# PSUM laid out by hand in the attention of a transformer block: three score tiles late, one bank for side work, chains two pairs ahead

## The chip, the core and the metric

The kernel runs on one core of one Trainium2 chip. A core has five engines that run side by side, each through its own instructions in order: TensorE (PE in the profile, its weight loads PEld), VectorE (DVE), ScalarE (ACT), GpSimd (POOL) and SyncE (SP, which here only issues DMAs). Work passes between them through SBUF (the large on-chip memory) and PSUM (where matmuls write). The metric is the device time of the whole kernel in microseconds; smaller is better.

## What is computed

A block of four layers over x of 4 sequences x 1024 tokens x 256 features, fp32, each with a layer norm ahead and a residual around it: attention, a mixture of experts, a causal convolution over the batch axis, and the same mixture again.

```python
x = x + _L0_attn_a_ref(_layernorm(x, axis=-1), L0_attn_a_w_qkv, L0_attn_a_w_out, L0_attn_a_ln_scale, L0_attn_a_ln_bias)
x = x + _L0_ffn_ref(_layernorm(x, axis=-1), L0_ffn_gate_w, L0_ffn_w1, L0_ffn_w2, L0_ffn_shared_w1, L0_ffn_shared_w2)
x = x + _L0_attn_b_ref(_layernorm(x, axis=-1), L0_attn_b_delta, L0_attn_b_alpha, L0_attn_b_beta, L0_attn_b_gamma)
x = x + _L0_ffn_ref(_layernorm(x, axis=-1), L0_ffn_gate_w, L0_ffn_w1, L0_ffn_w2, L0_ffn_shared_w1, L0_ffn_shared_w2)
```

The change is in the attention: 16 heads of 16 features, q and k rotated and normalised per head, and then weights that are the fourth power of the score instead of an exponential.

```python
def polynomial_attention(q, k, v, degree, is_causal):
    a = jnp.einsum('bhnd,bhmd->bhnm', q, k) ** degree
    if is_causal:
        a = jnp.tril(a)
    denom = jnp.sum(a, axis=-1, keepdims=True)
    return jnp.einsum('bhnm,bhmd->bhnd', a / denom, v)
```

The experts' part (16 experts, 6 per token, and a shared one) needs the tokens sorted by expert: the kernel scatters normalised rows into a queue in DRAM.

## The kernel before

**Passes and steps.** A sequence and a half of the heads (8 of 16) make a pair; there are 8 pairs. Queries come in two halves of 512 tokens (`hf`): first all 8 pairs with the early half, which sees keys of 4 blocks of 128, then all with the late half, which sees 8. One pair with one half is a pass (16 of them). A pass treats its 8 heads as two head-halves `a` of 4 heads, and for each walks over the key blocks `j`. So an early pass has 2 x 4 = 8 steps and a late one 2 x 8 = 16: 64 early steps and 128 late ones. Key blocks on the diagonal (the last four) are narrower and need a causal mask.

**One step.** `scores` (L686) lets PE multiply one key block with the queries of 4 heads into two PSUM tiles of 128 x 2 x 512 (L694); ACT squares both into SBUF (L705). On the diagonal DVE masks the first by a product (L712) and POOL the second (L714). Then the squares are squared again, to the fourth power: the first tile's on DVE (L725), the second's on ACT a step later (L863), some early ones on POOL (L727). `weigh` (L734) lets PE multiply these with v, with a column of ones for the sum, into an accumulator (L742). After the last block ACT copies that to SBUF (L751). Scores run `LOOK` = 2 steps ahead of weighing, in the main loop (L856).

**Side work in bites.** Everything else of the attention stage is cut into generators that run a piece at a time between the steps, in five lanes: `qkv_bites` of the pairs of either head group (L552; a chain of four projections, rotation, centring, square root, scaling, two times four transposes with an affine), `norm_bites` (the norm of x and its transposes), `gather_bites` with `project_bites` (division, output projection and residual), and a lane for routing (`prepare`, `plan`, `scatter`: norm, gate logits, top-k, slots and the 96 scatters of the first group). A generator yields `"pe"` ahead of a piece with matmuls, `"el"` ahead of one without, and `"gap"` where it wants to wait for the next step. `Bites.step(pe, counts)` runs at most so many pieces in each lane, and at most `pe` with matmuls in all. The loop calls it twice in a step, once after the scores and once after the weighing, both with `pe` = 1. `begin_chain(n)` starts the chain of pass n, `need` finishes it by force.

**What sets the order.** PE, DVE, ACT and SP keep the order in which the code is written; POOL's order comes from the scheduler of the framework. An engine waits for another through a semaphore, and everything behind a waiting instruction waits as well.

**PSUM.** Eight banks of 128 x 512 fp32: pool `ps_s` with two score tiles of two banks, `ps_a` with one accumulator, `ps_m` with three banks for bites, in both halves.

**Chains.** In the early half the chain of pass n + 2 begins at the middle of pass n, in the late half that of pass n + 1 at j = 3 of the first head-half of pass n. There is one v buffer for each pair of the early half, and two, used in turn, in the late one.

**After the attention.** The pools are given back and the experts' stage takes their memory: on SP loads of the shared experts' weights (L903, L906) and the gate and up weights (L911), on ACT loads of `w2a` and `w2b` (L918, L922), on DVE two memsets in `w2b` (L920, L921). Then the shared experts of the first group run (`shared`, L930), whose first matmuls (L955) need `hxT`, a transposed copy (L946), and only then the stream of routed tiles.

Of the kernel before, what the change touches and what calls it, by code (L numbers as in the profile page):

```python
# [8 lines left out]
FP = mybir.dt.float32  # L9
# [88 lines left out]
def chain(*parts):  # L98
    for part in parts:
        yield from part  # L100
# [3 lines left out]
def block_kernel(  # L104
# [342 lines left out]
    with ExitStack() as actx:  # L447
# [48 lines left out]
        def v_buffer(name):  # L496
            va = ap1.tile([P, 4, 8 * VW + 16], FP, name=name)
            nc.gpsimd.memset(va, 1.0)
            return va

        vA = [v_buffer(f"vA{i}") for i in range(len(pairs))]
        vB = [v_buffer(f"vB{i}") for i in range(2)]
        kA = [ap1.tile([P, 512], FP, name=f"kA{i}") for i in range(len(pairs))]


# [11 lines left out]
                    )  # L517

        qT, kT, vs_of, at_of, xnT_of = {}, {}, {}, {}, {}
        PS = {}  # L520

        def ps_m():
            return PS["m"]
# [1 line left out]
        def norm_bites(l, hf):  # L525

            xs = X[:, 4 * hf : 4 * hf + 4, l, :]
            yield "el"
            mv = small.tile([P, 4, 2], FP, tag="a_mv", name="a_mv")
            rstd = small.tile([P, 4], FP, tag="a_rstd", name="a_rstd")  # L530
            ln_stats(xs, mv, "a")
            yield "gap"
            yield "el"
            ln_root(mv, rstd)
            yield "gap"
            yield "el"
            nc.vector.reciprocal(rstd, rstd)
            xn = ap1.tile([P, 4, E], FP, name="xn")
            ln_apply(xs, xn, mv, rstd)
            xnT = ap2.tile([P, 2, 512], FP, name="xnT")  # L540
            xnT_of[l, hf] = xnT
            yield "gap"
            yield "gap"
            for k in range(2):
                yield "pe"
                pt = ps_m().tile([P, 512], FP, tag="m", name="pt")
                transpose4(pt, xn, slice(k * P, (k + 1) * P))
                nc.scalar.copy(xnT[:, k, :], pt)
# [3 lines left out]
        def qkv_bites(u, hf):  # L552
# [1 line left out]
            n = hf * len(pairs) + u  # L554
            l, gp = pairs[u]
            xnT = xnT_of[l, hf]
            va = vA[u] if hf == 0 else vB[u % 2]
            hd = D // 2
            full = [P, 2, 16, D]
            half = [P, 2, 16, hd]  # L560
# [125 lines left out]
        def scores(u, hf, a, j, last):  # L686

            n0 = max(0, (j - 4 * hf) * P)
            nq = 512 - n0
            kt = kT[u, j // 4]  # L690
            tiles = [PS["s"].tile([P, 2, 512], FP, tag="s", name="ps") for _ in range(2)]

            for h in (2, 0, 1, 3):
                nc.tensor.matmul(  # L694
                    tiles[h // 2][:, h % 2, 0:nq],
                    lhsT=kt[32 * h : 32 * h + 32, (j % 4) * P : (j % 4 + 1) * P],
                    rhs=qT[u, hf][a][32 * h : 32 * h + 32, n0:512],
                    start=True,
                    stop=True,
                )  # L700
            s2s, later = [], []
            masked = j >= 4 * hf
            for pr in range(2):
                s2 = sqp.tile([P, 2, 512], FP, name="s2")
                nc.scalar.activation(s2[:, :, 0:nq], tiles[pr][:, :, 0:nq], AF.Square)  # L705
                s2s.append(s2)
            for pr in range(2):
                s2 = s2s[pr]
                if masked:

                    if pr == 0:
                        nc.vector.tensor_mul(s2[:, :, 0:P], s2[:, :, 0:P], seen)  # L712
                    else:
                        nc.gpsimd.affine_select(  # L714
                            out=s2[:, :, 0:P],
                            in_=s2[:, :, 0:P],
                            compare_op=ALU.is_ge,
                            fill=0.0,
                            base=0,
                            pattern=[[0, 2], [1, P]],  # L720
                            channel_multiplier=-1,
                        )
                part = s2[:, :, 0:nq]
                if pr == 0 and (hf == 1 or j % 2 == 0):
                    nc.vector.tensor_mul(part, part, part)  # L725
                elif pr == 1 and hf == 0 and j % 2 == 1:
                    nc.gpsimd.tensor_mul(part, part, part)  # L727
                else:
                    later.append(part)
            return s2s, later  # L730

        accs = {}

        def weigh(u, hf, a, j, last, s2s):  # L734
            n0 = max(0, (j - 4 * hf) * P)
            if j == 0:
                accs[0] = PS["a"].tile([P, 512], FP, tag="acc", name="acc")
            acc = accs[0]
            va = vs_of[u, j // 4]
            for r in (2, 0, 1, 3):  # L740
                h = 2 * r + a
                nc.tensor.matmul(  # L742
                    acc[32 * r : 32 * r + 32, n0:512],
                    lhsT=va[:, j % 4, h * VW : h * VW + 32],
                    rhs=s2s[r // 2][:, r % 2, 0 : 512 - n0],
                    start=(j == 0),
                    stop=(j == last),
                )
# [82 lines left out]
        def forward(i):  # L831

            n, a, j, last = steps[i]
            hf, u = passes[n]
            if a == 0 and j == 0:
                bites.need(pairs[u][1], n)
            if hf == 0 and a == 1 and j == 0:
                begin_chain(n + 2)
            if hf == 1 and u > 0 and a == 0 and j == 3 and n + 1 < len(passes):

                begin_chain(n + 1)
            return scores(u, hf, a, j, last)

        with tc.manual_schedule(engines=ORDERED):
            with tc.tile_pool(name="ps_s", bufs=2, space=PSUM) as s, tc.tile_pool(
                name="ps_a", bufs=1, space=PSUM
            ) as a, tc.tile_pool(name="ps_m", bufs=3, space=PSUM) as m:
                PS.update(s=s, a=a, m=m)
                bites.add(NORM, norm_bites(0, 0), (0, 0))
                begin_chain(0)  # L850
                bites.need(QKV0, 0)
                begin_chain(1)
                bites.add(ROUTE, taps(ap1, ps_m))
                bites.add(ROUTE, zero_fill())
                routed = False
                for s in range(-LOOK, len(steps)):  # L856
                    bites.begin()
                    new = []
                    if s + LOOK < len(steps):
                        powers[s + LOOK], new = forward(s + LOOK)  # L860
                    bites.step(1, (1, 1, 1, 1, 1))
                    for part in later:
                        nc.scalar.activation(part, part, AF.Square)  # L863
                    later[:] = new
                    if s < 0:
                        bites.step(1, (2, 2, 1, 2, 1))
                        continue
                    n, a, j, last = steps[s]
                    hf, u = passes[n]
                    o_sb = weigh(u, hf, a, j, last, powers.pop(s))  # L870
                    bites.step(1, (2, 2, 1, 2, 1 if 0 not in plans or s % 2 else 0))
                    if o_sb is not None:
                        l, gp = pairs[u]
                        done = gather_bites(u, hf, a, o_sb)
                        if gp == 1 and a == 1:
                            done = chain(done, project_bites(l, hf))
                        bites.add(OUT, done)
                    if hf == 1 and not routed and not bites.lanes[OUT]:

                        routed = True  # L880
                        for i in range(TG):
                            bites.add(ROUTE, prepare(0, i, ap1, ps_m))
                        bites.add(ROUTE, chain(plan(0, ps_m), scatter(0, ap2, 1)))
                bites.drain(OUT)
                bites.drain(ROUTE)


    with ExitStack() as fctx:
# [432 lines left out]
```

## Time and profile before

| | us |
|---|---|
| median of 3 runs | 2390.59 (2389.18 to 2391.22) |
| the profiled execution, its run | 2393.24 |
| the profiled execution, its span | 2391.5 |
| attention, early half | 35 to 275 |
| attention, late half | 275 to 761 |
| shared experts of the first group | 761 to 855 |
| the rest (routed experts, convolution, experts again) | 855 to 2391.5 |

Busy in the whole span: PE 2114.5 us (88%), DVE 1118.5 (47%), ACT 1240.2 (52%), POOL 901.4 (38%). Mean granted clock of TensorE: 0.925.

How to read the lines of the profile that follow below: a group names line, engine, operation and output<-input, how often, and then busy time and mean duration in ns; after the bar stands the idle time of the engine ahead of it and what ended it. A line of the timeline begins with its start and length in us, and ends in brackets with the idle time and the releaser. A line of the waits names who waited for whom, us in total, times, and the longest.

### The profile page before, as it was taken

The page shows a single profiled execution, that of the slowest core. Times are in us where ns is not written, and L with a number is a line of the kernel's source. Part 1 is how long each engine was busy: PE and PEld are TensorE (multiplying, and loading weights), DVE is VectorE, ACT ScalarE, POOL GpSimd, SP SyncE. Part 2 cuts the span into 40 slices and gives each one's busy share as a digit, 9 for nine tenths or more (in the row PEclk, how much of TensorE's full clock was granted, in tenths as well). Part 3 has the DMA queues.
Part 4 walks back from the last instruction along what each step waited for, and adds up shares of the span by engine and source line. Part 5 has one row for each costly group of instructions (what it writes and reads, how often), then busy time and mean ns, then how long its engine had stood idle before and what let it go on. Part 6 is the DMA issues. An engine that isn't in the chain of part 4 may idle for free.

```text
span 2391.5 us, 33033 instructions
## 1 busy us (share of the span) xinstructions
PE 2114.5 (88%) x10480; PEld 1308.4 (55%) x10480; DVE 1118.5 (47%) x2532; ACT 1240.2 (52%) x2754; POOL 901.4 (38%) x990
## 2 busy tenths in 40 slices
PE   5899999778898998999899999789999959999974
PEld 2344443222233466777666667567676747777632
DVE  5888867656555225111166652126754212441154
ACT  3677878566676145555455544335553424555410
POOL 3333211344431000444355226645513654540176
PEclk8888988889888999999999999989999979999987
DMA  7900000111101412555455335344423535663243
GB/s 232 342 7 1 1 1 1 38 51 45 53 27 62 114 48 79 165 166 166 137 151 154 102 104 176 132 139 142 145 92 121 176 124 154 202 186 115 91 123 112
DMA packets 212231, 267.73 MB, mean 112 GB/s; under 512 B 25280, under 2 KB 187232, under 8 KB 212064
## 3 DMA queue, kind: packets, MB, share of 16 engines
q1 hardware_dynamic: 166944, 161.04, 21.6%
q0 software_dynamic: 36992, 100.78, 13.4%
q10 hardware_dynamic: 8128, 3.80, 0.7%
q8 instruction: 91, 1.49, 0.3%
q14 instruction: 76, 0.62, 0.1%
HBM read 123.72 MB, written 141.82 MB: 111 GB/s over the span
## 4 chain that ended last, share of the span: by engine, by line
PE 67%; DVE 12%; issue 7%; ACT 7%; POOL 5%; DMA 2%; ACTq 0%; POOLq 0%; DVEq 0%; SPq 0%
PE pgu L1030 20%; PE py L1053 14%; PE ps L694 6%; PE acc L742 4%; PE pxt L1014 4%; PE pht L1044 4%; POOL xq L421 3%; PE pg L955 3%; ACT s L705 3%; PE pj L571 3%; PE pu L955 3%; PE po L972 3%; POOL yg L1147 2%; ACT s L863 1%; DVE X L1131 1%
## 5 line engine op out<-in xcount | busy, mean ns | idle before, releaser
L421 POOL DMA_INDIRECT xq<-sxn,sloti x384 | 379.2, 987 | 644.7 <-ACT xgT L1016 306.2
L1030 PE MATMUL pgu<-wgu,xgT 128*128 x1776 | 609.7, 466 | 4.4 <-DVE hbuf L1039 2.2
L1147 POOL DMA_INDIRECT yg<-yq,sloti x384 | 375.8, 979 | 421.8 <-issue 201.4
L1039 DVE TENSOR_TENSOR hbuf<-hbuf,pgu 128x176 f32<-128x176 f32 x444 | 149.4, 337 | 721.7 <-ACT hbuf L1038 721.2
L1030 PEld LDWEIGHTS pgu<-wgu,xgT 128*128 128x128 f32 x1776 | 338.7, 193 | 136.5 <-issue 20.3
L1038 ACT ACTIVATE hbuf<-pgu 128x176 f32<-128x176 f32 x444 | 141.4, 318 | 411.7 <-PE pgu L1030 411.6
L705 ACT ACTIVATE s<-ps 128x1024 f32<-128x1024 f32 (+3 forms) x384 | 291.4, 815 | 114.6 <-PE ps L694 113.5
L1053 PE MATMUL py<-w2a,hT 128*128 x888 | 268.7, 385 | 0.9 <-ACT yo L1062 0.9
L1053 PE MATMUL py<-w2b,hT 128*128 x888 | 266.4, 382 | 0.0
L1062 ACT COPY yo<-py 128x256 f32<-128x256 f32 x444 | 166.1, 374 | 167.0 <-PE py L1053 166.7
L1131 DVE SCALAR_TENSOR_TENSOR X<-yg,top,X 128x256 f32<-128x256 f32 x384 | 186.0, 484 | 87.8 <-DMA yg<-yq,sloti 81.8
L1014 PE MATMUL pxt<-ident,xg 128*128 128x128 f32 x888 | 171.8, 276 | 60.6 <-DMA xg<-xq 60.6
L714 POOL TENSOR_SCALAR_AFFINE_SELECT s<-s 128x256 f32<-128x256 f32 x128 | 84.2, 659 | 349.7 <-ACT s L705 349.5
L725 DVE TENSOR_TENSOR s<-s 128x1024 f32<-128x1024 f32 (+3 forms) x160 | 168.2, 1051 | 86.8 <-ACT s L705 83.5
L1016 ACT COPY xgT<-pxt 128x256 f32<-128x256 f32 x444 | 167.9, 378 | 68.7 <-PE pxt L1014 68.3
L694 PE MATMUL ps<-q,kA 32*128 32x512 f32 (+3 forms) x1024 | 182.0, 647 | 20.0 <-ACT s L705 18.0
L1044 PEld LDWEIGHTS pht<-ident,hbuf 128*128 128x128 f32 x888 | 125.9, 142 | 124.4 <-issue 71.1
L1053 PEld LDWEIGHTS py<-w2b,hT 128*128 128x128 f32 x888 | 170.2, 192 | 23.5
L863 ACT ACTIVATE s<-s 128x1024 f32<-128x1024 f32 x192 | 164.4, 856 | 27.5 <-POOL s L714 27.2
L1044 PE MATMUL pht<-ident,hbuf 128*128 128x128 f32 x888 | 171.6, 275 | 4.9 <-ACT hT L1046 4.9
L1046 ACT COPY hT<-pht 128x256 f32<-128x256 f32 x444 | 165.4, 372 | 1.7 <-PE pxt L1014 0.7
L742 PE MATMUL acc<-s,vA 128*32 128x512 f32 (+3 forms) x1024 | 140.1, 603 | 13.2 <-ACT s L863 10.8
(158 smaller groups left out, 2421.9 us busy)
## 6 DMA issues: line engine op xcount, KB each, us to landing
xg<-xq SPq DMA_DIRECT2D x148, 384.0 KB, 3.7
yq<-yo SPq DMA_DIRECT2D x148, 384.0 KB, 2.8
xq<-zero SPq DMA_DIRECT2D x74, 384.0 KB, 4.6
xq<-sxn,sloti POOLq DMA_INDIRECT x384, 2.4
yg<-yq,sloti POOLq DMA_INDIRECT x384, 2.9
wgu<-in_w SPq DMA_DIRECT2D x4, 1408.0 KB, 17.8
X<-in_x SPq DMA_DIRECT2D x8, 512.0 KB, 5.5
out<-X SPq DMA_DIRECT2D x8, 512.0 KB, 3.5
```

The source lines that it names most:

```text
L421: d = nc.gpsimd.indirect_dma_start(out=xq[g][:, :], out_offset=bass.IndirectOffsetOnAxis(ap=sloti[:, c + i, k : k + 1], axis=0), in_=xs[:, ...
L694: nc.tensor.matmul(tiles[h // 2][:, h % 2, 0:nq], lhsT=kt[32 * h : 32 * h + 32, (j % 4) * P : (j % 4 + 1) * P], rhs=qT[u, hf][a][32 * h : ...
L705: nc.scalar.activation(s2[:, :, 0:nq], tiles[pr][:, :, 0:nq], AF.Square)
L725: nc.vector.tensor_mul(part, part, part)
L742: nc.tensor.matmul(acc[32 * r : 32 * r + 32, n0:512], lhsT=va[:, j % 4, h * VW : h * VW + 32], rhs=s2s[r // 2][:, r % 2, 0 : 512 - n0], st ...
L863: nc.scalar.activation(part, part, AF.Square)
L1014: nc.tensor.transpose(pt[:, k, :], xg[c][:, k * P : (k + 1) * P], ident)
L1030: nc.tensor.matmul(pg, lhsT=xT[c][:, k, :], rhs=wgu_f[k][:, bass.ds(vals[0] * (2 * FI), 2 * FI)], start=(k == 0), stop=(k == 1),)
L1044: nc.tensor.transpose(pt[:, k, :], hbuf[c % 4][:, k * P : (k + 1) * P], ident)
L1053: nc.tensor.matmul(py, lhsT=hT[c][:, k, :], rhs=w2_f[k][:, bass.ds(off[c] * E, E)], start=(k == 0), stop=(k == 1),)
L1131: nc.vector.scalar_tensor_tensor(X[:, t, l, :], yg[:, k, :], top[:, i, k0 + k : k0 + k + 1], X[:, t, l, :], op0=ALU.mult, op1=ALU.add,)
L1147: nc.gpsimd.indirect_dma_start(out=yg[:, k, :], out_offset=None, in_=yq[g][:, :], in_offset=bass.IndirectOffsetOnAxis(ap=sloti[:, i, k0 + ...
```

## The change

Three parts. PSUM is laid out by hand: three score tiles, one bank `sums` and one bank `spare`. In the early half two score tiles are used, and bites rotate over `spare` and the two banks of the third tile; in the late half the three score tiles are used in turn (`turn`), and bites have `spare` alone. In the late half the first call of `step` gets `pe` = 0, so that a step runs at most one bite with matmuls, after the weighing. The fourth power of the second tile moves from ACT to DVE in the late half for j = 1 and 3. Late chains begin two passes ahead (at j = 6 of the second head-half of pass n for pass n + 2), with three v buffers in turn. The main loop keeps its content and loses a level of indentation.

```diff
-        vB = [v_buffer(f"vB{i}") for i in range(2)]
+        vB = [v_buffer(f"vB{i}") for i in range(3)]
...
+        pp = actx.enter_context(tc.tile_pool(name="psum", bufs=1, space=PSUM))
+        score_tiles = [pp.tile([P, 2, 512], FP, name=f"sc{i}") for i in range(3)]
+        sums = pp.tile([P, 512], FP, name="sums")
+        spare = pp.tile([P, 512], FP, name="spare")
+
+        class Banks:
+            def __init__(self, banks):
+                self.banks, self.n = banks, 0
+            def tile(self, shape, dtype, tag=None, name=None):
+                bank = self.banks[self.n % len(self.banks)]
+                self.n += 1
...
+                view = bank[:, 0:size]
...
+                return view
+
+        early = Banks([spare, score_tiles[2][:, 0, :], score_tiles[2][:, 1, :]])
+        late = Banks([spare])
+        PS = {"m": early}
+        turn = [0]
...
-            va = vA[u] if hf == 0 else vB[u % 2]
+            va = vA[u] if hf == 0 else vB[u % 3]
...
-            tiles = [PS["s"].tile([P, 2, 512], FP, tag="s", name="ps") for _ in range(2)]
+            tiles = []
+            for _ in range(2):
+                tiles.append(score_tiles[turn[0] % (2 if hf == 0 else 3)])
+                turn[0] += 1
...
-                if pr == 0 and (hf == 1 or j % 2 == 0):
+                if pr == 0 and (hf == 1 or j % 2 == 0) or hf == 1 and j in (1, 3):
                     nc.vector.tensor_mul(part, part, part)
...
-            if j == 0:
-                accs[0] = PS["a"].tile([P, 512], FP, tag="acc", name="acc")
-            acc = accs[0]
+            acc = sums
...
-            if hf == 1 and u > 0 and a == 0 and j == 3 and n + 1 < len(passes):
-
-                begin_chain(n + 1)
+            if hf == 1 and a == 1 and j == 6 and n + 2 < len(passes):
+
+                begin_chain(n + 2)
+            if hf == 1:
+                PS["m"] = late
...
-                    bites.step(1, (1, 1, 1, 1, 1))
+                bites.step(0 if PS["m"] is late else 1, (1, 1, 1, 1, 1))
```

More of the change, by code (lines that the diff above doesn't have):

```diff
@@ L519, in block_kernel @@
         qT, kT, vs_of, at_of, xnT_of = {}, {}, {}, {}, {}
-        PS = {}
+        pp = actx.enter_context(tc.tile_pool(name="psum", bufs=1, space=PSUM))
[8 more added lines that the diff above has]
+                self.n += 1
+                size = 1
+                for d in shape[1:]:
+                    size *= d
+                view = bank[:, 0:size]
+                if len(shape) == 3:
+                    view = view.rearrange("p (a b) -> p a b", b=shape[2])
+                elif len(shape) == 4:
+                    view = view.rearrange("p (a b c) -> p a b c", b=shape[2], c=shape[3])
+                return view
[3 more added lines that the diff above has]
+        turn = [0]
         def ps_m():
@@ L730, in scores @@
             return s2s, later
-        accs = {}
         def weigh(u, hf, a, j, last, s2s):
             n0 = max(0, (j - 4 * hf) * P)
-            if j == 0:
-                accs[0] = PS["a"].tile([P, 512], FP, tag="acc", name="acc")
-            acc = accs[0]
+            acc = sums
             va = vs_of[u, j // 4]
@@ L838, in forward @@
                 begin_chain(n + 2)
-            if hf == 1 and u > 0 and a == 0 and j == 3 and n + 1 < len(passes):
-                begin_chain(n + 1)
+            if hf == 1 and a == 1 and j == 6 and n + 2 < len(passes):
+                begin_chain(n + 2)
+            if hf == 1:
+                PS["m"] = late
             return scores(u, hf, a, j, last)
         with tc.manual_schedule(engines=ORDERED):
[L845 to L860, printed above, removed]
-                    bites.step(1, (1, 1, 1, 1, 1))
[L862 to L885, printed above, removed]
@@ new lines, in block_kernel @@
+            bites.add(NORM, norm_bites(0, 0), (0, 0))
+            begin_chain(0)
+            bites.need(QKV0, 0)
+            begin_chain(1)
+            bites.add(ROUTE, taps(ap1, ps_m))
+            bites.add(ROUTE, zero_fill())
+            routed = False
+            for s in range(-LOOK, len(steps)):
+                bites.begin()
+                new = []
+                if s + LOOK < len(steps):
+                    powers[s + LOOK], new = forward(s + LOOK)
+                bites.step(0 if PS["m"] is late else 1, (1, 1, 1, 1, 1))
+                for part in later:
+                    nc.scalar.activation(part, part, AF.Square)
+                later[:] = new
+                if s < 0:
+                    bites.step(1, (2, 2, 1, 2, 1))
+                    continue
+                n, a, j, last = steps[s]
+                hf, u = passes[n]
+                o_sb = weigh(u, hf, a, j, last, powers.pop(s))
+                bites.step(1, (2, 2, 1, 2, 1 if 0 not in plans or s % 2 else 0))
+                if o_sb is not None:
+                    l, gp = pairs[u]
+                    done = gather_bites(u, hf, a, o_sb)
+                    if gp == 1 and a == 1:
+                        done = chain(done, project_bites(l, hf))
+                    bites.add(OUT, done)
+                if hf == 1 and not routed and not bites.lanes[OUT]:
+                    routed = True
+                    for i in range(TG):
+                        bites.add(ROUTE, prepare(0, i, ap1, ps_m))
+                    bites.add(ROUTE, chain(plan(0, ps_m), scatter(0, ap2, 1)))
@@ L888, in block_kernel @@
+            bites.drain(OUT)
+            bites.drain(ROUTE)
     with ExitStack() as fctx:
```

## The prediction

> **What bounds the kernel now.** I read the busy times of each engine in three stretches first, then the chain of waits, then the late half step by step.
>
> ```profile
> 35.00:275.00 240.00, 217.24 (x1400) 94.48 (x1396) 198.03 (x376) 171.97 (x297) 85.70 (x114) 0.89 0.38 125
> 275.00:761.00 486.00, 416.93 (x2496) 146.40 (x2492) 297.76 (x535) 354.43 (x485) 149.17 (x173) 0.87 0.08 27
> 761.00:855.00 94.00, 83.39 (x257) 46.19 (x258) 28.40 (x46) 14.68 (x26) 0.00 (x0) 0.91 0.42 112
> ...
> 400.00:447.00 47.00, 42.53 (x252) 16.07 (x248) 43.40 (x71) 36.80 (x50) 4.13 (x7) 0.97 0.00 1
> 447.00:475.00 28.00, 19.01 (x92) 5.01 (x84) 10.99 (x19) 11.59 (x16) 17.63 (x19) 0.63 0.19 69
> ```
>
> Columns: stretch, its length, then busy us of PE, weight loads, DVE, ACT and POOL, TensorE clock, DMA share, GB/s. Attention is 35 to 761 us: the early half to 275, the late half 486 us for 128 steps. The shared experts then run to 855 us. After 761 us the change touches nothing but when the stage may begin. In the chain of waits PE carries two thirds:
>
> ```profile
> PE 67%; DVE 12%; issue 7%; ACT 7%; POOL 5%; DMA 2%; ACTq 0%; POOLq 0%; DVEq 0%; SPq 0%
> ```
>
> In the late half that is PE and ACT by turns. ACT is idle for 486.0 - 354.4 = 131.6 us there, and its list of waits says for what:
>
> ```profile
> ACT s L705 <- PE ps L694: 79.9, 72, 3.3
> ACT s L863 <- POOL s L714: 27.2, 8, 8.3
> ACT h_vs L662 <- DVE h_vs L620: 11.8, 6, 3.9
> ```
>
> The first is the two score tiles: a step without extra work takes 3.2 us (first squarings start at 736.50 and 739.66). ACT squares for 1.94 us, and only after its second squaring may three of four score matmuls start (the weight loads at 738.49):
>
> ```profile
> 737.57 0.29 PEld L694 LDWEIGHTS ps<-q,kA 32*128 32x128 f32 x2 [1.04 <-ACT s L705]
> 738.49 0.31 PEld L694 LDWEIGHTS ps<-q,kA 32*128 32x128 f32 x6 [0.62 <-ACT s L705]
> ```
>
> The second is POOL, which runs 12 scatters of 0.97 us (1.27 apart) ahead of a causal mask:
>
> ```profile
> 583.53 0.96 POOL L421 DMA_INDIRECT xq<-sxn,sloti  x1 [0.30 <-issue]
> 584.50 0.78 POOL L714 TENSOR_SCALAR_AFFINE_SELECT s<-s 128x256 f32<-128x256 f32 x2
> 584.96 1.06 ACT L863 ACTIVATE s<-s 128x1024 f32<-128x1024 f32 x1 [4.86 <-POOL s L714]
> ```
>
> The third is ACT's square root for the head norm, which stands in ACT's order behind DVE's centring. Last, how the next stage begins:
>
> ```profile
> 767.39 0.37 SPq L903 DMA_DIRECT2D sh<-in_shared_w  x1
> 767.39 0.47 ACTq L918 DMA_DIRECT2D w2a<-in_w  x1
> ...
> 768.94 3.47 DVE L920 MEMSET w2b<- 32x4096 f32 x1 [0.91 <-issue]
> 772.83 1.07 ACT L946 COPY hxT<-hpt 128x512 f32<-128x512 f32 x2 [8.86 <-DVE w2b L920]
> 773.47 0.50 PEld L955 LDWEIGHTS pg<-hxT,sh 128*128 128x128 f32 x2 [4.52 <-ACT hxT L946]
> ```
>
> The last mask ends at 759.6 us, and the shared experts' first matmul is 13.9 us later.
>
> **What the Trainium skill says.** "Perfetto Trace Analysis", Optimization Strategy: a gap that repeats on the engine that should be full can mean too little PSUM for the next tile. The trace agrees (79.9 us in 72 waits). "PSUM — Partial Sum Buffer", Specifications: 8 banks of 512 fp32 values per partition; three score tiles of two banks, the sums and the spare fill them, so bites can have only one. "TensorE: Matmul & The Clock Gate", What's actually happening: an idle TensorE falls to half clock after about 3.4 us. The trace agrees: 0.63 in the stretch with scatter stalls, 0.97 in the one before.
>
> **The late half, part by part.** Prices, from the rows and the timeline: four full score matmuls 1.07 us, weighing 1.0, one projection bite 1.49, transposes 0.6; ACT pair of squarings 1.83 start to start, fourth power 0.95, copy of a projection 0.36, of the sums 0.47, an affine 0.67; DVE square 1.22, rotation 2.08, centring 2.9, root's inverse and scaling 1.84.
>
> With three tiles a step's scores need only the first squaring of the step before: the loop is 1.07 + 0.12 + 1.0 + 0.05 = 2.25 us instead of 3.2. The fourth powers of j = 1 and 3 leave ACT (32 x 1.07 = 34 us) and join DVE (32 x 1.22 = 39 us). I walked one typical pass (odd pair, chain of the pair after next beside it) through the changed order, starts of first squarings:
>
> - Second head-half: 2.85, 4.6, 2.25, 2.8, 2.1, 2.35, 3.15 and 3.4 us for j = 0 to 7, 23.5 us. ACT sets j = 0 to 5, the two projection bites the last.
> - First head-half: j = 0 takes 3.2. Then DVE has, without a pause, double square 2.44, rotation 2.08, square 1.22, centring 2.9, output division 0.7, double square 2.44, rotation 2.08, mask and square 1.68, centring 2.9 = 18.4 us, from 1.0 after the start of j = 1. ACT's root is due after 3.6 + 2.8 + 2.8 + 2.25 + 1.4 = 12.9 us and gets its input at 19.4: it waits 6.5 us. PE idles 6 us, so what follows (two weighings, two score groups) is partly at half clock and takes 7.2 us. Sum 29.8.
>
> That is 53.3 us, where the two odd passes before took 63.4 and 61.1, scatter stalls included. The other passes by the same walk, before and then after: pair 0 54.4, 47; pair 1 62.8, 57.5; pair 2 70.5, 60; pair 3 63.4, 58.5; pair 4 65.3, 69.5; pair 5 61.1, 60.5; pair 6 59.7, 55; pair 7 46.8, 41.5. Pair 4 gets slower since routing, with a single PE bite per step, comes there instead of in pair 2: its top-k and one-hot work (9 us) falls on the DVE stretch that already binds. Scatter stalls (27.2 us before) shrink to about 8, as masks and scatters alternate in shorter groups. Sum 484 before, 449.5 after; 2.5 for joins I did not walk: **saving 32 us**. Bounds: 15 (clock low in every root wait, DVE slowed beside POOL) to 60 (the waits of 6.5 us mostly hidden).
>
> **The scatters that are left.** In the changed order 22 of the 96 scatters stand on POOL behind the last mask; before, none did. The shared weights' load on SP, w2a's on ACT and the memset of w2b on DVE now name these scatters in their waits, as their memory was the scatter's source. Behind SP's load stand the other weights, behind ACT's the copy of hxT, and DVE's order has both memsets and hxn behind the first. So: 22 x 1.27 = 27.9, landing 2.4, memsets 0.9 + 3.5 + 0.9 + 3.5, small ones and hxn 2, transposes at half clock 1.2, copy 0.6 and hand-overs: about 42.3 us from mask to first shared matmul, where it was 13.9. **Cost 28 us**, all on the path, since PE has nothing else; the single bank's slower last output projection hides under it. Bounds 24 to 33 (1.27 is the pace without DVE beside it; 12 took 16.7 us in one busy group).
>
> **The early half.** Bites rotate over the spare bank and both banks of the third tile, but the waits in the changed order hold that tile as one: a bite in one of its banks waits until the bite in the other is read. Mostly the reader is done. Where it isn't: the second output projection beside pair 7 waits for an addition that DVE has behind its centring (6.3 us instead of 2.5: 3.8), outputs beside pairs 3 and 5 wait 1.0 and 1.7, a projection for the affine of queries 1.7, smaller ones 1. **Cost 9 us**; bounds 2 (absorbed in waits for DVE of 4.3 us, as in pairs 4 and 6) and 14.
>
> The third v buffer and its memset, the loop of names and the sums in a fixed bank cost nothing: the memset (0.6 us, one more of 10) lies in the start where POOL is idle, and the sums had one buffer already.
>
> **Sum.** -32 + 28 + 9 = +5 us on the execution's span of 2391.5, so 2396.5; that execution took 2393.2 where the median is 2390.6, so I name 2396 for the median.
>
> **Rivals.**
> 1. DVE's backlog does not bind: place, the square root in j = 5 of a first head-half; price 6.5 us and 3 us of slow clock in six passes. If most is hidden, the late half saves 60 and the time is 2391.5 - 60 + 37 = 2368. For it: DVE is only 61% busy in the late half, and ACT loses its largest wait. Against: one such root already waits 3.9 us before, with 15 us of DVE work ahead; now there are 18.4. It decides once the late half saves more than 37.
> 2. The third tile gives little: root waits, cold TensorE and routing in the wrong place leave a saving of 15, the shared bank costs 12 and the scatters 28: 2391.5 + 25 = 2416. For it: the clock of 0.63 after stalls. Against: in pairs 0 and 7, with little or no chain, the tile loop alone is worth 5 to 7 us a pass.
> 3. The tail of scatters is hidden (in part the saving of the new layout itself): then 2391.5 - 32 + 9 = 2368 as well. Against: the waits are named in the order, on three engines; I give it little.
>
> **How the numbers follow.** Forecast (2384 to 2406) 0.53, rival 1 and 3 together 0.29, rival 2 0.18. A difference below 0.2% (4.8 us) cannot be told from none here. The forecast's own spread puts some 0.03 below, 0.17 inside and 0.33 above it: faster 0.32, same 0.17, slower 0.51. The range takes in most of both rivals: 2370 to 2415. The forecast's own is 2384 to 2406.
>
> **What would show it.** Right: late half near 452 us, ACT's wait for score matmuls under 30 us, roots waiting some 40 us in all; clock dips just after them; 22 scatters after the last mask, the first shared matmul about 42 us after it; early half 5 to 12 us longer, PE waiting for readers of the third tile. Wrong: roots that wait under 3 us each, or shared weights landing before the last scatter.

## The result and the profile after

| | before | after |
|---|---|---|
| median, us | 2390.9 (2389.2 to 2392.5) | 2406.8 (2405.1 to 2409.2) |
| span of the profiled execution | 2391.5 | 2407.5 |
| first squaring of attention | 35.8 | 38.2 |
| early half: from there to the first late squaring | 239.4 | 262.5 |
| late half: from there to the first squaring of its last step | 483.2 | 440.5 |
| last causal mask to the first matmul of the shared experts | 13.9 | 44.7 |
| that matmul | 773.5 | 789.6 |
| from it to DVE's last addition, the end here | 1614.2 | 1614.1 |

The changed kernel is slower: ratio 1.0067, 95% interval 1.005 to 1.0085. The whole difference lies ahead of the shared experts' first matmul, 16.1 us later, and it is a sum of large terms: start +2.4 (36.6 in e4_powers_back below, which edits late steps alone, so this wanders by 2 us), early half +23.1, late half -42.7, the last mask 2.5 us late behind two scatters, the tail +30.8.

The same stages in the windows of the changed kernel (stretch, length, then busy us of PE, weight loads, DVE, ACT and POOL, clock, DMA share, GB/s):

```profile
38.20:300.70 262.50, 208.49 (x1400) 91.95 (x1404) 199.15 (x381) 173.77 (x297) 89.78 (x114) 0.91 0.33 110
300.70:744.90 444.20, 349.76 (x2484) 125.12 (x2484) 330.92 (x559) 321.75 (x451) 147.22 (x150) 0.91 0.06 23
744.90:789.60 44.70, 13.00 (x45) 8.58 (x45) 11.26 (x16) 2.76 (x5) 21.12 (x22) 0.53 0.41 145
```

The early half has the work it had (PE 208 us, DVE 199, ACT 174), in 23 us more: these are waits. In the late half ACT does 33 us less and DVE 33 more, the moved fourth powers; the clock is 0.91, and was 0.87. In the tail only POOL has much to do.

ACT's waits in the late half, where before had 79.9, 27.2 and 11.8 us:

```profile
ACT s L737 <- PE sc L726: 67.0, 60, 5.7
ACT h_vs L691 <- DVE h_vs L649: 31.9, 7, 8.6
ACT s L890 <- POOL s L746: 7.0, 5, 3.5
```

The roots wait, 31.9 us in all where some 40 were forecast, and the scatters hardly hold up masks any more. One of the roots in the timeline, pair 5:

```profile
606.42 0.69 DVE L649 TENSOR_REDUCE h_vs<-m 128x32 f32<-128x512 f32 x1
607.14 0.35 ACT L691 ACTIVATE h_vs<-h_vs,eps_t 128x64 f32<-128x64 f32 x1 [8.57 <-DVE h_vs L649]
...
610.99 1.06 ACT L890 ACTIVATE s<-s 128x1024 f32<-128x1024 f32 x1 [3.50 <-POOL s L746]
612.10 1.94 PE L770 MATMUL sums<-s,vB 128*32 128x512 f32 x8 [8.20 <-ACT s L890]
```

ACT stands 8.57 us for the sum of squares, then 3.5 for a mask behind scatters. PE stands 8.2 us, and its next eight weighing records take 1.94 us, where the same eight take 1.07 at 739.65 us. This agrees with "TensorE: Matmul & The Clock Gate" of the Trainium skill (What's actually happening), by which a TensorE that has stood idle runs at half its clock at first: the granted clock is 0.76 from 590 to 617 us and 0.99 in the 23 us after.

PE's waits in the early half, longest sums first. Left out at the dots are those that before had too, and others of up to 2.1 us in all:

```profile
PE sc L245 <- DVE at L797: 8.1, 2, 5.4
...
PE sc L600 <- ACT qkv L607: 4.6, 6, 1.4
...
PE sc L822 <- DVE X L830: 3.8, 1, 3.8
PE sc L792 <- DVE X L830: 2.8, 2, 1.6
...
PE sc L726 <- DVE at L797: 2.4, 1, 2.4
```

One of those left out has grown: the scores' wait for ACT's squarings (PE sc L726 <- ACT s L737) is 7.8 us, and was 2.4. It is 9.0 us in the kernel below that wins the early half back, so it is not what costs the time.

"sc" is now also what bites write. The first line is the clearest: L245 is the broadcast of a convolution tap, L797 the division of an attention output. They share no data. The timeline beside pair 1:

```profile
108.71 0.66 PE L792 MATMUL sc<-ident,o_sb 128*128 128x128 f32 x4
110.81 1.68 DVE L200 TENSOR_SCALAR xn<-X,a_mv,a_rstd 128x256 f32<-128x256 f32 x4
115.02 0.42 DVE L797 TENSOR_TENSOR at<-sc,rd 128x256 f32<-128x256 f32 x1
115.50 1.22 PE L245 MATMUL sc<-diag,ones 128*128 128x128 f32 x4 [5.35 <-DVE at L797]
118.85 1.94 ACT L737 ACTIVATE s<-sc 128x1024 f32<-128x1024 f32 x2 [7.83 <-PE sc L726]
```

The output's transposes at 108.71 fill one bank of the third tile. DVE reads it at 115.02 only, behind a centring, a layer norm, a mask and a rotation. The tap goes to the other bank, and waits 5.35 us all the same; the next scores stand behind it in PE's order, so ACT is without work for 7.83 us.

The chain of waits as a whole

```profile
PE 50%; DVE 6%; issue 4%; POOL 4%; DMA 3%; ACT 1%; POOLq 0%; DVEq 0%; ACTq 0%; SPq 0%
```

adds to 68%, some 1630 us: followed back from the end it reaches the last scatter and goes no further. Its oldest pieces are the tail (start, length, what):

```profile
775.21 2.37 DMA xq<-sxn,sloti
778.82 3.47 DVE w2b L947
...
783.20 3.47 DVE w2b L948
...
787.13 0.26 DVE hxn L200
787.48 2.25 PE hpt L182 x8
789.73 2.88 PE pg L982 x4
```

The last scatter lands at 777.6, two memsets and the norm follow on DVE, then the transposes and the first shared matmul.

### The profile page after: what moved, and what is told of

It is laid out like the page before. It is cut to its first block, busy times and chain, and to the rows that moved or that the text cites. A ratio compares the mean times of both kernels' runs of the same rounds, so it can differ in the third digit from the quotient of the medians.

```text
span 2407.5 us, 33032 instructions
## 1 busy us (share of the span) xinstructions
PE 2048.6 (85%) x10480; PEld 1290.1 (54%) x10480; DVE 1153.5 (48%) x2564; ACT 1210.0 (50%) x2722; POOL 924.2 (38%) x991
## 3 DMA queue, kind: packets, MB, share of 16 engines
q1 hardware_dynamic: 166944, 161.04, 21.4%
## 4 chain that ended last, share of the span: by engine, by line
PE 50%; DVE 6%; issue 4%; POOL 4%; DMA 3%; ACT 1%; POOLq 0%; DVEq 0%; ACTq 0%; SPq 0%
PE pgu L1057 19%; PE py L1080 14%; PE pxt L1041 4%; PE pht L1071 3%; PE pg L982 3%; PE pu L982 2%; PE po L999 2%; POOL yg L1174 2%; DMA yg<-yq,sloti 1%; DVE X L1158 1%; POOL xq L421 1%; PE pl L289 1%; PE hpt L182 1%; PE fpt L182 1%; DMA xq<-sxn,sloti 1%
## 5 line engine op out<-in xcount | busy, mean ns | idle before, releaser
L421 POOL DMA_INDIRECT xq<-sxn,sloti x384 | 388.1, 1011 | 590.4 <-ACT xgT L1043 305.4
L737 ACT ACTIVATE s<-sc 128x1024 f32<-128x1024 f32 (+3 forms) x384 | 291.2, 815 | 115.3 <-PE sc L726 114.7
L746 POOL TENSOR_SCALAR_AFFINE_SELECT s<-s 128x256 f32<-128x256 f32 x128 | 92.7, 726 | 386.3 <-ACT s L737 376.9
L757 DVE TENSOR_TENSOR s<-s 128x1024 f32<-128x1024 f32 (+1 forms) x192 | 201.6, 1064 | 75.9 <-ACT s L737 72.5
L770 PE MATMUL sums<-s,vA 128*32 128x512 f32 (+3 forms) x1024 | 128.6, 559 | 37.8 <-ACT o_sb L779 14.0
L726 PE MATMUL sc<-q,kA 32*128 32x512 f32 (+3 forms) x1024 | 134.3, 591 | 16.9 <-ACT s L737 12.7
L1041 PEld LDWEIGHTS pxt<-ident,xg 128*128 128x128 f32 x888 | 112.6, 143 | 61.8 <-issue 61.1
```

The lines of the kernel that those rows point to most:

```text
L421: d = nc.gpsimd.indirect_dma_start(out=xq[g][:, :], out_offset=bass.IndirectOffsetOnAxis(ap=sloti[:, c + i, k : k + 1], axis=0), in_=xs[:, ...
L1041: nc.tensor.transpose(pt[:, k, :], xg[c][:, k * P : (k + 1) * P], ident)
```

## The experiments

They ran in three groups, each on one chip. On the chips of the first two groups the kernel before takes 2479 and 2475 us, and there 1679 to 1695 us pass from the first shared matmul to the end in every kernel, instead of 1614: in stages that no edit touches. (The end is DVE's last addition, as above.) So I use the ratio to the kernel before on the same chip, and of the traces the times up to that matmul. "Late half" runs to the first squaring of its last step; pairs 0 to 3 and 4 to 7 are its parts; tail is last mask to first shared matmul.

| kernel | group | ratio (95%) | early | late | pairs 0-3 | pairs 4-7 | tail | first shared matmul |
|---|---|---|---|---|---|---|---|---|
| before | - | 1 | 239.4 | 483.2 | 251.1 | 232.2 | 13.9 | 773.5 |
| after | - | 1.0067 (1.005, 1.0085) | 262.5 | 440.5 | 215.7 | 224.7 | 44.7 | 789.6 |
| e1_early_apart | 1 | 0.9968 (0.9954, 0.9982) | 241.5 | 452.6 | 215.6 | 237.1 | 43.4 | 777.8 |
| e2_two_bites | 1 | 1.0124 (1.0089, 1.016) | 262.6 | 490.4 | 267.8 | 222.6 | 18.1 | 810.7 |
| e3_two_tiles | 1 | 1.009 (1.0054, 1.0125) | 261.5 | 459.6 | 224.8 | 234.8 | 43.4 | 805.6 |
| e4_powers_back | 1 | 1.0019 (1.0007, 1.003) | 264.9 | 435.8 | 214.2 | 221.7 | 43.5 | 784.5 |
| a2_changed | 2 | 1.0098 (1.0064, 1.0131) | 263.3 | 450.0 | 215.9 | 234.2 | 43.1 | 798.4 |
| e5_own_rows | 2 | 0.9982 (0.9961, 1.0003) | 262.7 | 451.3 | 215.7 | 235.7 | 22.7 | 778.7 |
| e6_apart_own | 2 | 0.9893 (0.9857, 0.9929) | 241.9 | 453.2 | 215.7 | 237.5 | 21.4 | 756.1 |
| e8_one_ahead | 2 | 1.0081 (1.0052, 1.0109) | 265.2 | 478.1 | 207.6 | 270.6 | 21.4 | 803.6 |
| e10_all_but_powers | 3 | 0.9854 (0.984, 0.9869) | 244.4 | 440.2 | 215.5 | 224.7 | 17.1 | 741.3 |
| e9_all | 3 | 0.9821 (0.9801, 0.9841) | 241.4 | 433.0 | 216.1 | 216.8 | 17.6 | 732.8 |
| e11_all_slow | 3 | 0.9967 (0.9954, 0.998) | 240.6 | 448.6 | 216.3 | 232.4 | 14.4 | 748.1 |
| e12_all_slow_one | 3 | 0.9872 (0.9855, 0.989) | 241.4 | 448.6 | 204.8 | 243.9 | 15.4 | 742.7 |

(On the third group's chip the kernel before takes 2393.0 us.)

**e1_early_apart.** The early half's two borrowed banks as tiles of their own:

```diff
-score_tiles = [pp.tile([P, 2, 512], FP, name=f"sc{i}") for i in range(3)]
+score_tiles = [pp.tile([P, 2, 512], FP, name=f"sc{i}") for i in range(2)]
...
-early = Banks([spare, score_tiles[2][:, 0, :], score_tiles[2][:, 1, :]])
+ectx = ExitStack()
+pe = ectx.enter_context(tc.tile_pool(name="ps_e", bufs=1, space=PSUM))
+early = Banks([spare] + [pe.tile([P, 512], FP, name=f"bank{i}") for i in range(2)])
...
-if hf == 1:
+if hf == 1 and PS["m"] is early:
     PS["m"] = late
+    ectx.close()
+    pl = actx.enter_context(tc.tile_pool(name="ps_l", bufs=1, space=PSUM))
+    score_tiles.append(pl.tile([P, 2, 512], FP, name="sc2"))
```

> The changed kernel, with the two banks that the early half's bites borrow as two tiles of one bank each; the third score tile is made in their place when the late half begins. Order of work and the tail of 22 scatters unchanged. Theory A (early loss of 23 us is the two banks being held as one tile): the waits of PE's bites for readers of the other bank (taps 5.4 and 2.8, second output projection 3.8, and the others of 1 to 2.5 us) vanish, the early half takes 239 to 244 us in place of 262.5, total 2382 to 2388. Rival B (the loss is the fixed turn of the two score tiles, or the order of the chains): early half stays at 258 or more, total 2403 or more.

Theory A holds for the early half: 241.5 us, 21 less, same order of work. (In e10_all_but_powers, with the same edit, the two longest single waits there of PE for a reader of a bite's bank are:

```profile
PE sc L728 <- DVE at L799: 3.3, 1, 3.3
PE bank L182 <- DVE xn L200: 2.5, 1, 2.5
```

Lines lie two further down; the norm's 2.5 us were there before the change. The taps' waits, the second output projection's 3.8 us and those for copies of q, k and v are gone. What stays of the sharing is the first late score, 3.3 us, which takes over memory a bite was read from.) By the ratios it is 1% or a little more faster than the changed kernel. Its trace showed the late half 12 us longer, in pairs 5 and 6 alone; a2_changed was to tell whether that is the edit.

**e2_two_bites.** Two PE bites a step in the late half, as before, on the one bank:

```diff
-bites.step(0 if PS["m"] is late else 1, (1, 1, 1, 1, 1))
+bites.step(1, (1, 1, 1, 1, 1))
```

> The changed kernel, with two PE bites a step allowed in the late half again, on the one spare bank. Routing's plan comes earlier and no scatter is left behind the last mask. Theory A (the tail of scatters lies wholly on the path): last mask to first shared matmul 14 to 17 us in place of 44.7, late half no more than 6 us longer, total 2377 to 2386. Rival C (a second bite of a step waits on the one bank for its reader, and scatters come back in front of masks): late half 15 us or more longer, total 2393 or more.

The tail shrank nearly as theory A said (18.1 us, where it had 14 to 17), and yet the theory fell: the late half is 50 us longer, all of it in pairs 0 to 3. With two bites a step routing's plan is done early, and its scatters begin at 469 us, in pair 2. ACT's waits from 301 to 792 us:

```profile
ACT s L737 <- PE sc L726: 78.7, 50, 11.4
ACT s L890 <- POOL s L746: 56.3, 18, 5.5
```

In pairs 0 to 3 alone masks behind scatters hold up ACT for 23.7 us. PE also waits there for readers of the one bank, 7.0 us of it for copies of projections, a wait that the changed kernel does not have. Rival C named both and holds; which of them costs more is not shown. The lesson is that tail and late half trade with each other.

**e3_two_tiles.** The third tile left unused in the late half:

```diff
-tiles.append(score_tiles[turn[0] % (2 if hf == 0 else 3)])
+tiles.append(score_tiles[turn[0] % 2])
```

> The changed kernel, with the late half's scores on two tiles in turn; the third tile lies unused there. All else unchanged. Theory A (the third tile makes most of the late saving of 43 us): late half 25 to 40 us longer, ACT's waits for score matmuls up again by some 30 us, total 2432 to 2447. Rival D (the chains two pairs ahead and the fourth powers moved to DVE make it): late half at most 10 us longer, total 2407 to 2417.

In between: 19 us longer than after, of which 9.1 lie in pairs 0 to 3, 7.9 in pair 7, and 2.2 in pairs 4 to 6. PE's wait from 299 to 760 us shows the mechanism, the scores waiting for ACT's squaring:

```profile
PE sc L726 <- ACT s L737: 57.2, 66, 3.1
```

With three tiles that line has 5.5 us. ACT's own wait for scores is 76.0 us here against 67.0, so it rises by 9 us and not by theory A's 30. By the time of the whole kernel it cannot be told from a2_changed (1.009 and 1.0098, overlapping intervals). So the third tile makes less than half of the late saving. In pairs 0 to 3, where the changed kernel saves 35.4 us, it makes 9.

**e4_powers_back.** The second fourth power of steps 1 and 3 of a late head-half on ACT again:

```diff
-if pr == 0 and (hf == 1 or j % 2 == 0) or hf == 1 and j in (1, 3):
+if pr == 0 and (hf == 1 or j % 2 == 0):
```

> The changed kernel, with the second fourth power of steps 1 and 3 of a late head-half on ACT again. Theory A (ACT sets the pace where no chain runs; DVE's backlog costs less than the 34 us of squarings do on ACT): late half 5 to 20 us longer though roots wait 10 to 20 us less, total 2412 to 2427. Rival E (DVE's backlog binds: the 32 us of waits at the root and PE's 12.8 us for DVE's squares go): late half 5 to 20 us shorter, total 2387 to 2402.

Theory A fell, and the sign is rival E's: the late half is 4.7 us shorter than after's, just under its 5 to 20, and the ratio is 0.8% below a2_changed's. That move of the change loses.

**a2_changed**, the changed kernel unedited, in the second group:

> The changed kernel once more, unedited, so that the runs beside it can be set against it on the same chip. Theory A: first shared matmul at 786 to 790 us, ratio to the kernel before 1.005 to 1.0085 as measured first. Rival F (the late half's length wanders by 10 us from one execution to the next, as the 452.6 us of e1_early_apart against 440.5 might mean): late half outside 437 to 444 us.

The late half took 450.0 us here, outside 437 to 444 as rival F had it, and the first shared matmul came at 798.4, not at theory A's 786 to 790. Pairs 0 to 4 equal the first trace within 0.2 us each, and pair 5 takes 66.5 us instead of 60.4. So of the 11 to 13 us that e1, e5 and e6 show in pairs 5 to 7, 9.5 come with no edit at all: stalls on these two chips (last section). In the third group e10, which has the edits of e6 and one more, takes 440.2.

**e5_own_rows.** The rows that scatters read, in memory that outlives attention:

```diff
-xs = pool.tile([P, 2, E], FP, tag="sxn", name="sxn")
+xs = rt2.tile([P, 2, E], FP, tag="sxn", name="sxn")
```

> The changed kernel, with the rows that the scatters read in a pool that outlives attention, so that no load or memset of the next stage takes their memory. The 22 scatters stay behind the last mask. Theory A (they are on the path only since the weights' loads and the memset wait for their memory): last mask to first shared matmul 15 to 21 us in place of 44.7, first shared matmul at 762 to 767 us, total 24 to 29 us less than the changed kernel. Rival G (the tail is the single bank's last output projection, 16 us from the last mask to its last addition, and DVE's memsets): first shared matmul at most 15 us earlier; or the first expert tile, which reads the scattered rows, waits, and the gain is lost there.

The same 22 scatters stand behind the last mask, the last of them ending at 787.6 us, and the first shared matmul starts at 778.7: 22.7 us after the mask instead of 43.1, and by the ratio the kernel is 1.2% faster than the changed one. So the scatters were on the path through the reuse of their memory alone. It missed 21 us at the upper end, since what they covered now shows:

```profile
766.81 0.69 DVE L830 TENSOR_TENSOR X<-X,spare 128x512 f32<-128x512 f32 x1 [2.97 <-PE spare L822]
767.55 3.78 PE L822 MATMUL spare<-wout_sb,aT 128*128 128x256 f32 x8 [0.85 <-DVE X L830]
771.37 0.69 DVE L830 TENSOR_TENSOR X<-X,spare 128x512 f32<-128x512 f32 x1 [3.88 <-PE spare L822]
771.47 0.37 SPq L930 DMA_DIRECT2D sh<-in_shared_w  x1
778.02 1.07 ACT L973 COPY hxT<-hpt 128x512 f32<-128x512 f32 x2 [15.15 <-DMA sh<-in_shared_w]
```

The second half of attention's last projection waits on the one bank for the first half's addition. Its matmuls end 15.4 us after the mask, and only then, at 771.47, is the load of the shared weights issued. The bracket of the last line names that load, but ACT also issues the load of `w2b` just ahead of this copy, at 777.12, and this comes right after DVE's first memset of `w2b` (773.62 to 777.09).

**e6_apart_own.** e1 and e5 together.

> Both: the early half's bites in two one-bank tiles, and the scatters' rows in a pool that outlives attention. Theory A (two separate costs): first shared matmul at 737 to 745 us, 44 to 52 us before the changed kernel's, total 1.4 to 1.9% under it and 0.8 to 1.3% under the kernel before. Rival F (what the early half gains is lost in the late half, as e1_early_apart's trace had it): first shared matmul at 750 us or later.

The time is theory A's: 1.07% under before, 1.9% under a2_changed. The profiled execution's first shared matmul, 756.1, is on rival F's side of 750; its late half of 453.2 us has the stalls of that chip, which a2_changed has without the edits. The two costs are separate and add.

**e8_one_ahead.** Late chains started one pair ahead, as before:

```diff
-if hf == 1 and a == 1 and j == 6 and n + 2 < len(passes):
-    begin_chain(n + 2)
+if hf == 1 and u > 0 and a == 0 and j == 3 and n + 1 < len(passes):
+    begin_chain(n + 1)
```

> The changed kernel, with each late chain started where the kernel before starts it (the next pair's, at the fourth step of a first head-half, from the second pair on), in place of two pairs ahead. Banks, tiles, one PE bite a step and fourth powers as changed. Theory A (the third tile and the early chains share the late saving; without them the chain ends as a lump before its pair): late half 8 to 30 us longer than 440.5. Rival H (the early start is worth nothing, the saving is the third tile's 19 us and the single bite of a step): late half within 5 us of 440.5, or shorter.

The size is theory A's (478.1, 28 us more than a2_changed), its reason is not. No chain ended as a lump: pairs 0 to 3 are 8 us shorter than with the early start, and roots wait 11.5 us instead of 31.9. All the loss is in pairs 4 to 7. ACT's wait for masks up to 761 us:

```profile
ACT s L890 <- POOL s L746: 48.4, 7, 10.9
```

To the half's end at 781 us it is 55.5. Here 84 of the scatters stand in seven groups of 12, each ahead of a mask, with none left behind the last. So the early start pays in the late half, as far as these runs show, by delaying routing and breaking up these groups. For the whole kernel it brings nothing: with no scatter behind the last mask the tail is 21.4 us instead of 43.1, and the ratio of 1.0081 cannot be told from a2_changed's 1.0098.

**e10_all_but_powers and e9_all.** e6, and the last drain of outputs on four banks; e9 has e4's edit as well:

```diff
+PS["m"] = Banks([spare] + [t[:, 0, :] for t in score_tiles])
 bites.drain(OUT)
```

> Early banks as two tiles, the scatters' rows in a pool that outlives attention, and the last output projection of attention on the spare bank and one bank of each score tile in turn (no scores are left then). Fourth powers as in the changed kernel. Theory A: the last projection's bites no longer wait for their readers, last mask to first shared matmul 15 to 19 us in place of the 21.4 of e6_apart_own, ratio to the kernel before 0.984 to 0.990. Rival I (the loads' landing ends it, not the projection): 20 us or more, ratio as e6_apart_own's 0.9893.

> e10_all_but_powers with the second fourth power of steps 1 and 3 of a late head-half on ACT again. Rival E, which e4_powers_back spoke for (DVE's backlog binds): 5 to 15 us less than e10_all_but_powers, late half 435 to 445 us, roots wait under 25 us in all. Theory A as first held: 5 to 20 us more than e10_all_but_powers.

Both forecasts of e10 by theory A hold: tail 17.1, ratio 0.9854. e9 is a further 7.6 us faster (2351.7 against 2359.3, same chip): rival E again, with a late half of 433.0 us, 7.2 less than e10's and 2 under its range. ACT's waits there, first e10's, then e9's:

```profile
ACT s L739 <- PE sc L728: 68.3, 60, 6.7
ACT h_vs L693 <- DVE h_vs L651: 32.1, 7, 8.6
```

```profile
ACT s L739 <- PE sc L728: 45.3, 39, 6.0
ACT h_vs L693 <- DVE h_vs L651: 22.3, 6, 7.6
```

With 32 fourth powers more to do, ACT waits 33 us less and finishes earlier: it had been waiting anyway, 32.1 us of it for DVE at the roots. (DVE is not without waits either; for ACT's squarings it waits over 100 us of the late half in both kernels.) e9_all beats both kernels, 1.8% under before. Its stages:

```profile
37.20:278.60 241.40, 207.21 (x1400) 90.25 (x1404) 201.05 (x381) 171.70 (x298) 86.89 (x114) 0.91 0.36 123
278.60:715.20 436.60, 343.99 (x2484) 123.01 (x2480) 291.89 (x527) 348.79 (x483) 143.05 (x150) 0.93 0.07 23
715.20:732.80 17.60, 9.14 (x45) 6.78 (x45) 9.40 (x12) 2.85 (x6) 13.45 (x14) 0.69 0.57 194
```

**e11_all_slow and e12_all_slow_one.** e9 with one scatter a step, and that with chains one pair ahead:

```diff
-bites.step(1, (2, 2, 1, 2, 1 if 0 not in plans or s % 2 else 0))
+bites.step(1, (2, 2, 1, 2, 1 if 0 not in plans else 0))
```

> e9_all with one scatter a step once routing's plan stands, where it was one in one step and two in the next, so that more are left behind the last mask, where nothing waits for their memory. Theory J (scatters beside the late half cost it POOL waits and stalls of all engines of some 5 to 15 us): late half 5 to 15 us shorter than e9_all's, first expert tile no later after the first shared matmul than the 77 us there. Rival K (the added tail of scatters delays the first expert tile, or what they cost does not depend on their pace): total as e9_all or above.

> e11_all_slow with each late chain started where the kernel before starts it, one pair ahead. Theory L (the start two pairs ahead brings the late half nothing by itself; e8_one_ahead was 8 us shorter in pairs 0 to 3 and lost only by groups of 12 scatters ahead of masks): late half as e11_all_slow or up to 15 us shorter. Theory A (it is part of the saving): 8 us longer or more.

e11 went the other way: late half 15.6 us longer. POOL's order, which is not written by hand, still gathers up to 12 scatters and sets masks behind them:

```profile
ACT s L895 <- POOL s L748: 29.1, 8, 5.3
```

(e9 has 7.7 us.) And with 36 scatters behind the last mask the first expert tile starts 91.9 us after the first shared matmul, not 78.6: rival K on both counts. In e12 pairs 0 to 3 are 11.5 us shorter than e11's, pairs 4 to 7 as much longer: theory L for the chains themselves, and again the scatters' place decides the rest. The whole kernel is 21 us faster than e11 (2362.4 against 2383.3): 24 scatters are left behind the last mask instead of 36, and from the first shared matmul to the end it takes 1614.1 us instead of 1631.6. One pair ahead at e9's own pace of scatters was not run.

## Why the prediction came out as it did

- **Direction, and the tail: right.** Cost 28 us forecast (its terms add to 42.9 us and not to the 42.3 given, which changes little), 30.8 measured; first shared matmul 42.3 us after the last mask forecast, 44.7 measured; 22 scatters. The mechanism is shown by e5, which removes it without moving a scatter. The extra is a pause I left out: POOL waits 3.9 us for the last rows, whose norm stands in DVE's order behind the last addition.
- **The total: near, by some luck.** Forecast +5 us on the span, measured +16.0; the median of 2406.8 lies just above the forecast's own 2384 to 2406. The early half cost 14.1 us more than forecast, and the late half saved 10.7 us more, which made up for most of it; start, last mask and tail add 7.7. And the range of 2370 to 2415 leaves the centres of both rivals, 2368 and 2416, just outside, though the prediction says that it takes in most of both.
- **The early half: the term that failed.** "Cost 9 us", bounds 2 to 14; measured 23.1, and 2.4 at the start. The mechanism, two banks held as one tile, was right: with tiles apart the half takes 240.6 to 244.4 us in six kernels. The step that failed is the list: "Mostly the reader is done" and "smaller ones 1". The ones I named measured 3.8 (the second output projection), 2.8 (outputs behind additions, where I had 1.0 and 1.7) and 1.4 (a projection for queries): 8.0 in all. Not on the list were the taps, 8.1 us in two waits, the first late score, 2.4, the projections' waits for copies, 4.6, and waits of 1 to 2 us for transposed norms and keys. (These waits overlap in part, and so add to more than the 23.1 us.) I had looked for bites with a late reader in the pairs' own chains, and passed over the lane of the taps, which runs in the first two pairs only.
- **The late half: right in form, 10.7 us short.** Forecast saving 32, measured 42.7. Every pair came within 4.3 us (47.4, 54.0, 57.2, 57.1, 65.2, 60.4, 55.0, 44.1 against 47, 57.5, 60, 58.5, 69.5, 60.5, 55, 41.5), pair 4 slowest. Roots waited 31.9 us for some 40, masks 7.0 for about 8. Pairs 1 to 4 were each charged 1.4 to 4.3 us too much, and the 2.5 us for joins were not there.
- **What the saving is: only partly what I gave as its reason.** I derived the gain from the loop of 2.25 us instead of 3.2 and said routing comes to pair 4 instead of pair 2. e3, e2 and e8 show the proportions: the third tile is worth 19 us at most, and in pairs 0 to 3 9.1 of 35.4. The other 26 go, in all likelihood, with routing's scatters leaving these pairs, since only one bite a step is let through: before, ACT waits 18.2 us for masks there and the clock is 0.86, after it has no such wait and the clock is 0.94. With two bites (e2) the pairs take 267.8 us, but there PE waits for the one bank as well, so no run shows this share by itself. The chains two pairs ahead do not make it: without them (e8) pairs 0 to 3 are shorter still, 207.6 us. A part of this gain is the very work that comes back as the tail.
- **A wrong sign.** "ACT's wait for score matmuls under 30 us" was 67.0. I took the fourth powers on DVE as 34 us off ACT against 39 on DVE, in a half where the roots already waited for DVE. e9 against e10 prices the move: 7.6 us lost. Even without it the wait is 45.3, so the bound of 30 was wrong for other reasons too.
- **Rivals.** The first was to decide once the late half saved more than 37. It saved more, with the roots waiting as in the forecast, so its mechanism was not what happened. The second's total came nearest (2416, in which the shared bank costs 12), but by a late half that saves 15. The third, a hidden tail, is what e5 had to build.

## What to carry to other kernels

When tiles are laid out by hand, ask what the waits take as one tile: a pair of banks lent to two users ties each to the other's reader, and here a split of the tile alone was worth 21 us. When a stage gets faster, look which work has moved behind it, and whether the next stage's loads reuse that work's memory; 4 KB per partition kept apart turned 31 us of added tail into 9, and spare banks at the end took off some 4 more. Before moving work to the engine with the lower busy share, look whether the other engine is already waiting for it.

## What the runs showed that I had not expected

"Perfetto Trace Analysis" of the Trainium skill (Matmuls) advises rotating independent matmul groups through different PSUM banks, so that the reading of one overlaps the matmuls of the next. This trace agrees only where the banks are separate tiles: rotation over two banks of one tile did not overlap them (5.35 us in the first case), for a reason of the waits and not of the memory, as e1 shows.

Chips differ in the untouched stages: 1614 to 1618 us from the first shared matmul to the end in five kernels (before, after, and three of the last group; 1631.6 in e11, whose first expert tile is late), 1679 to 1695 in the eight of the first two groups. On their chips, PE and ACT also stop beside scatters in pairs 5 and 6 with no releaser among the engines; e1_early_apart:

```profile
602.25 0.58 ACT L781 COPY o_sb<-sums 128x512 f32<-128x512 f32 x1 [1.21 <-remote]
602.89 1.06 PE L772 MATMUL sums<-s,vA 128*32 128x512 f32 x8 [2.51 <-issue]
611.01 1.94 ACT L739 ACTIVATE s<-sc 128x1024 f32<-128x1024 f32 x2 [3.19 <-remote]
```

Their cause was not tried, and stays open.
